# Graph convolution with a sparse adjacency on one core: the unit of the first columns comes two places later in the order of the units

## The chip, the cores and the metric

The kernel runs on one core of a Trainium2 chip. The metric is the device time of one execution in microseconds (us); the median of the runs counts.

## The reference

Only what matters of it is shown. There are 8 batches of 4096 nodes with 256 features; `adj` is 4096 x 4096 and sparse, denser towards the first rows and columns: the chance of an entry falls with the root of both indices.

```python
HW = jnp.einsum('bnf,fo->bno', H, W)
A_norm = jax.nn.relu((A + A.T) * 0.5)
D = jnp.sum(A_norm, axis=1)
D_safe = jnp.where(D > 0, D, 1.0)
d_inv_sqrt = jnp.where(D > 0, D_safe ** (-0.5), 0.0)
DAD = d_inv_sqrt[:, None] * A_norm * d_inv_sqrt[None, :]
L_norm = jnp.eye(N, dtype=H.dtype) - DAD
out = jnp.einsum('nm,bmo->bno', L_norm, HW)
return jax.nn.relu(out)
# around it: x = _layernorm(x + that, axis=-1)
```

## The kernel before

It has two halves. The first builds what the second multiplies; everything is in 32-bit floats.

**Building (lines 691 to 748).** The adjacency is read in blocks of 512 x 512, made symmetric with transposes on PE, cut at zero and written to `a_dram`. Beside it the features are multiplied by `w` and scaled with the root of the degrees; the result `g`, one row of 2048 values (8 KB: 8 batches of 256) for each node, goes to `g_dram`. A flag for each node and each group of 32 columns says whether there is an entry at all (`uses`). The product for the first 128 output rows (`lead`) is made here already.

**Multiplying (lines 885 to 1256).** The 31 other blocks of 128 output rows go in 16 *units*: unit `u` has the blocks 2u+1 and 2u+2, unit 15 only the last one. So unit 0 holds the first, densest columns after `lead`. For a unit only those rows of `g` are fetched that have an entry in its columns. They are sorted by *kind*, which is the pattern of the eight groups of 32 columns that a row has entries in; the tables `CAPS` and `FIRST` give each kind a number of half tiles of 64 rows, and the place of the first. This gives each unit its number of gathered tiles of 128 rows: 22, 19, 19, 18, 17, 17 and 16 for the units 1 to 7, 27 for unit 0, and 17, 16, 14, 15, 15, 13, 13 and 10 for the units 8 to 15.

`steps_of(u)` (line 818) makes the unit's list of PE steps. A full step multiplies a whole tile, or one of two fixed hub tiles of the first 256 nodes, into one block. A tiled step, or round, packs up to eight products of 64 rows by 32 columns, taken from up to five neighbouring tiles, side by side on the array. Both take four column slices of 512. Steps by unit: 21, 18, 17, 15, 15, 14 and 13 for the units 1 to 7, 28 for unit 0, and 12, 12, 12, 12, 11, 11, 11 and 4 for 8 to 15. A tile can be needed in several rounds.

What sets the order:

- `SEQ` (line 24) is the order of the units. `steps` (line 904) strings their steps together in it, and `order` (line 905) the tiles by first use.
- `gather(n)` (line 936) fetches tile n with two indirect DMAs on POOL's queue: the weights out of `a_dram` (line 943) and the rows of `g` (line 951; up to 1 MB). Tiles lie in a ring of `RING = 12` slots. `gather_ahead` (line 961) counts off slots strictly in order: a tile is gone only when all tiles before it are used up too, and its slot is what tile n + 12 waits for.
- While a unit runs, the lists of later ones are made: `ahead` (line 1083) takes, from the places two, three and four further in `SEQ`, the unit whose indices are spread out (`spread`), the unit whose leftover rows are placed (`place_rest`), and the unit whose patterns are found (`patterns`, `place`). This is DVE work with a few small matmuls in between (`lists`, line 1100), which stand in PE's order near the end of the unit.
- Each finished block is evicted from PSUM by ACT (line 759), added to its block of `x`, normalised on DVE and stored (line 812, SP's queue); the `x` blocks are loaded on ACT's queue (line 753). These start some steps into the next unit (`after`, lines 1199 to 1208).
- `queue(engine)` chains what each engine gets in the order of the program.
- In the building half `SEQ` gives the place at which the constants of each unit are set (line 648), and the first four units, whose lists are begun there (lines 730 and 737).

Of the kernel before, what the change touches and what calls it, by code (L numbers as in the profile page):

```python
# [20 lines left out]

KINDS = [15, 1, 4, 2, 8, 16, 64, 32, 128, 240, 51, 204, 60, 195, 0]

SEQ = [1, 2, 3, 4, 5, 6, 7, 0, *range(8, 16)]

HUBS = [*[2] * 15, 0]

# [40 lines left out]
def kernel(  # L68
# [49 lines left out]
    def blocks(u):  # L118

        return min(2, NB - 1 - 2 * u)  # L120
# [349 lines left out]
    with (  # L470
# [176 lines left out]

        due = [[n + 1, constants, (u,)] for n, u in enumerate(SEQ)]

# [29 lines left out]
        def spread_early(u):  # L679
            hot = spool.tile([P, A, S], F32, tag="sym", name=f"hot_{u}")  # L680
            mixed = blocks_pool.tile([P, A, S], F32, tag="adj", name=f"mixed_{u}")
            mixed = mixed.rearrange("p a s -> p (a s)")
            n = NB * tmax
            return spread(
                u,
                hot.rearrange("p a s -> p (a s)").bitcast(BF16).rearrange("p (m q) -> p m q", q=P),
                mixed[:, : n // 2].bitcast(BF16).rearrange("p (m t) -> p m t", t=tmax),
                mixed[:, n : 2 * n].bitcast(BF16).rearrange("p (m k t) -> p m k t", k=2, t=tmax),
            )

        for i in range(NS):
# [37 lines left out]
            if i in (1, 2):  # L729
                for n, u in enumerate(SEQ[2 * i - 2 : 2 * i]):  # L730
                    at = 1 + 5 * n
# [4 lines left out]
            elif i in (3, 4):  # L736
                pieces = spread_early(SEQ[i - 3])
                due += [[at, next, (pieces, None)] for at in (1, 2, 3, 3, 4)]
                due.append([5, collect_index, (SEQ[i - 3],)])
            due.sort(key=lambda d: d[0])  # L740
# [10 lines left out]
    def residual(i, engine):  # L751
        xr = blocks_pool.tile([P, B, F], F32, tag="adj", name=f"xr_{i}")
        engine.dma_start(xr, x[:, i * P : (i + 1) * P, :].rearrange("b p f -> p b f"))
        return xr
# [130 lines left out]
    with (  # L885
# [17 lines left out]
        stat = gath.enter_context(tc.tile_pool(name="stat", bufs=3))  # L903
        steps = [(u, step) for u in SEQ for step in steps_of(u)]
        order = list(dict.fromkeys((u, op[0]) for u, step in steps for op in step if op[0] >= 0))
# [81 lines left out]

        u = SEQ[0]
        xr = {i: residual(i, nc.sync) for i in (0, *range(2 * u + 1, 2 * u + 1 + blocks(u)))}
# [330 lines left out]
```

## Time and profile before

| | |
|---|---|
| median of 3 runs | 1507.45 us (1506.8 to 1508.42) |
| the profiled execution, its own time | 1505.85 us |
| its span, first to last instruction | 1503.7 us |
| mean granted clock of PE | 0.968 |
| indirect DMAs of rows of `g` (line 951) | 268 |
| moved by DMA | 543.04 MB, mean 361 GB/s |
| units, first product to last product | 591.7 to 1484.9 us |

The span is what the profile sees of the execution's own time; 2.2 us lie around it. PE is TensorE, PEld its weight loads, DVE VectorE, ACT ScalarE, POOL GpSimd and SP SyncE. A wait is written as the waiting instruction, an arrow, and who ended the wait. The DMA share is the mean busy share of 16 DMA engines; packets of several queues that overlap can put it a little over 1.

### The profile page before, as it was taken

To read this page: it belongs to the slowest core of one execution; us is meant where nothing else is said; L and a number is where in the kernel's file an instruction comes from. 1 tells how busy PE (TensorE), PEld (TensorE's weight loads), DVE (VectorE), ACT (ScalarE), POOL (GpSimd) and SP (SyncE) were. 2 spreads that over 40 slices of the span, in tenths; PEclk is the share of its full clock that TensorE was granted. 3 is DMA by queue.
4 is the path that set the end of the run, shared out by engine and by line. 5 is a ranking of instruction groups with operands and counts; after the bars stand their busy time and mean duration, and the time that the engine had idled before them with its cause. 6 is when DMAs were issued, how large, how long until landed. Compare 5 with 4: busy or idle time off the path is not lost.

```text
span 1503.7 us, 29689 instructions
## 1 busy us (share of the span) xinstructions
PE 1387.0 (92%) x11008; PEld 751.7 (50%) x11008; DVE 1040.8 (69%) x3173; ACT 361.2 (24%) x462; POOL 773.3 (51%) x1564
## 2 busy tenths in 40 slices
PE   6999998989999988999999999999999998988983
PEld 5877876767777763343433333333333333433431
DVE  5676668979956462319486897789229897999644
ACT  3555554444444451000101101100010010011111
POOL 3444010011213225775775777777566776777762
PEclk9999999999999989999999999999999999999996
DMA  9999999999989999999999999999979999999994
GB/s 358 366 364 398 399 376 360 367 330 354 356 311 348 332 397 379 394 400 332 373 379 358 375 398 379 382 388 384 366 255 343 343 374 401 374 368 391 379 370 144
DMA packets 217158, 543.04 MB, mean 361 GB/s; under 512 B 19369, under 2 KB 109193, under 8 KB 182425
## 3 DMA queue, kind: packets, MB, share of 16 engines
q0 software_dynamic: 55664, 283.87, 48.8%
q1 hardware_dynamic: 93472, 126.89, 24.6%
q10 hardware_dynamic: 67872, 130.32, 23.1%
q8 instruction: 89, 1.46, 0.4%
q14 instruction: 61, 0.50, 0.1%
HBM read 438.03 MB, written 136.34 MB: 382 GB/s over the span
## 4 chain that ended last, share of the span: by engine, by line
PE 52%; DMA 19%; DVE 19%; issue 5%; POOL 3%; ACT 2%; ACTq 0%; SPq 0%; POOLq 0%; DVEq 0%
PE py L1158 33%; DMA g<-g_dram,gi 9%; PE pg L606 9%; DMA a_dram<-sym 4%; DVE sym L499 3%; PE lead L564 3%; PE tr L495 3%; PE xtr L595 3%; DVE sums L506 3%; DMA ga<-a_dram,ai 2%; DMA xin<-in_x_dram 2%; DVE stats L778 1%; POOL ga L943 1%; DVE xr L769 1%; DVE xr L802 1%
## 5 line engine op out<-in xcount | busy, mean ns | idle before, releaser
L1158 PE MATMUL py<-g,ga 64*32 64x512 f32 (+1 forms) x7136 | 619.9, 609 | 29.1 <-DMA g<-g_dram,gi 24.8
L1158 PEld LDWEIGHTS py<-g,ga 64*32 64x32 f32 (+1 forms) x7136 | 226.9, 113 | 405.7 <-issue 323.2
L951 POOL DMA_INDIRECT g<-g_dram,gi x268 | 306.4, 1143 | 115.7 <-issue 67.4
L943 POOL DMA_INDIRECT ga<-a_dram,ai x268 | 285.9, 1067 | 137.4 <-PE py L1158 65.2
L759 ACT ACTIVATE y<-py,minus_r 128x512 f32<-128x512 f32 x120 | 72.8, 688 | 793.5 <-PE py L1158 562.8
L606 PE MATMUL pg<-w_sb,xt 128*128 128x256 f32 x1024 | 229.5, 382 | 5.8 <-ACT xt L596 4.0
L1158 PE MATMUL py<-g_hub,gh 128*128 128x512 f32 x480 | 222.1, 604 | 3.9 <-DVE pos_k L239 3.9
L499 DVE TENSOR_TENSOR sym<-tr,adj 128x512 f32<-128x512 f32 x256 | 161.5, 680 | 81.1 <-PE tr L495 80.1
L606 PEld LDWEIGHTS pg<-w_sb,xt 128*128 128x128 f32 x1024 | 194.0, 192 | 33.6 <-ACT xt L596 4.4
L507 POOL TENSOR_SCALAR uses<-sums 128x64 uint8<-128x64 f32 x64 | 27.7, 433 | 311.3 <-DVE sums L506 262.8
L506 DVE TENSOR_REDUCE sums<-sym 128x64 f32<-128x2048 f32 x64 | 145.3, 2276 | 51.7 <-ACT sym L503 51.7
L495 PE MATMUL tr<-ident,adj 128*128 128x128 f32 x1024 | 139.7, 287 | 28.6 <-DVE sym L499 16.6
L1158 PEld LDWEIGHTS py<-g_hub,gh 128*128 128x128 f32 x480 | 88.0, 190 | 132.7 <-issue 119.8
L503 ACT ACTIVATE sym<-sym 128x2048 f32<-128x2048 f32 x64 | 122.8, 1918 | 126.5 <-DVE sym L499 126.5
L495 PEld LDWEIGHTS tr<-ident,adj 128*128 128x128 f32 x1024 | 119.7, 147 | 55.3 <-DVE sym L499 34.1
L442 DVE TENSOR_SCALAR low<-lists 128x17 f32<-128x17 f32 (+8 forms) x14 | 2.5, 175 | 197.9 <-PE lists L430 193.3
L769 DVE TENSOR_TENSOR xr<-xr,y 128x2048 f32<-128x2048 f32 x31 | 70.8, 2284 | 52.7 <-ACT y L759 47.1
L595 PE MATMUL xtr<-ident,xin 128*128 128x128 f32 x512 | 73.9, 292 | 14.5 <-DVE sym L499 14.0
L802 DVE TENSOR_SCALAR xr<-xr,mv,root 128x256 f32<-128x256 f32 x248 | 85.6, 416 | 1.1
L778 DVE BATCH_NORM_STATS2 stats<-xr 128x6 f32<-128x256 f32 x248 | 84.1, 412 | 1.1
L564 PE MATMUL lead<-gt,strip 128*128 128x512 f32 x176 | 82.6, 593 | 0.0
L596 ACT COPY xt<-xtr 128x512 f32<-128x512 f32 x128 | 67.9, 593 | 45.1 <-PE xtr L595 44.0
(157 smaller groups left out, 1056.7 us busy)
## 6 DMA issues: line engine op xcount, KB each, us to landing
adj<-in_adj_dram SPq DMA_DIRECT2D x64, 1024.0 KB, 12.1
a_dram<-sym ACTq DMA_DIRECT2D x64, 1024.0 KB, 10.0
out_dram<-xr SPq DMA_DIRECT2D x31, 1024.0 KB, 17.5
xr<-in_x_dram ACTq DMA_DIRECT2D x28, 1024.0 KB, 18.4
xin<-in_x_dram SPq DMA_DIRECT2D x44, 512.0 KB, 10.5
g_dram<-gt ACTq DMA_DIRECT2D x22, 1024.0 KB, 7.6
xin<-in_x_dram POOLq DMA_DIRECT2D x20, 512.0 KB
g_dram<-held ACTq DMA_DIRECT2D x10, 1024.0 KB, 11.7
```

The costliest lines, as they stand in the source:

```text
L495: ins = nc.tensor.transpose(pt[:, c * P : (c + 1) * P], tji[:, c, a * P : (a + 1) * P], ident)
L499: nc.vector.tensor_add(sym[:, a, :], pt, tij[:, a, :])
L503: nc.scalar.activation(sym, sym, AF.Relu, scale=0.5)
L506: nc.vector.tensor_reduce(sums, sym.rearrange("p a (c q) -> p a c q", q=E), AX.X, ALU.add)
L564: nc.tensor.matmul(lead[c], lhsT=strip, rhs=g[:, c * S : (c + 1) * S], start=not done, stop=len(done) == NB - 1, skip_group_check=True,)
L595: nc.tensor.transpose(pt[:, k, c, :], xin[b // H][:, b % H + k, c * P : (c + 1) * P], ident)
L606: ins = nc.tensor.matmul(pg[:, k * FO : (k + 1) * FO], lhsT=xt[:, b + k, c, :], rhs=w_sb[:, c, :], start=(c == 0), stop=(c == FC - 1),)
L778: nc.vector.bn_stats(stats[:, b, :], z[:, b, :])
L802: nc.vector.tensor_scalar(z[:, b, :], z[:, b, :], mv[:, b, 0:1], rstd[:, b : b + 1], ALU.subtract, ALU.mult,)
L943: nc.gpsimd.indirect_dma_start(out=at if both else at[:, : E if one else P], out_offset=None, in_=a_pairs if both else a_groups if one els ...
L951: nc.gpsimd.indirect_dma_start(out=gt, out_offset=None, in_=g_dram, in_offset=bass.IndirectOffsetOnAxis(ap=gi[:, t : t + 1], axis=0), boun ...
L1158: return nc.tensor.matmul(py[2 * u + 1 + b][c][cols, :], lhsT=at[ps, off + cols.start : off + cols.stop], rhs=gt[ps, c * S : (c + 1) * S], ...
```

## The change

Unit 0 moves from the eighth place of the order to the tenth: the order was 1 to 7, 0, 8 to 15, and is 1 to 9, 0, 10 to 15. The units 8 and 9 come one unit 0 earlier, behind unit 7; behind unit 0 now stands unit 10. Nothing else is edited. Through `SEQ` this reorders the steps, the gathers, the preparation of lists and, in the building half, the place at which the constants of 8, 9 and 0 are set.

```diff
-SEQ = [1, 2, 3, 4, 5, 6, 7, 0, *range(8, 16)]
+SEQ = [*range(1, 10), 0, *range(10, 16)]
```

## The prediction

> **What bounds the kernel now.** I read the page first (busy time, slices, chain), then the stretches of the units, then the gap that these show, at its queue.
>
> The page says that no engine is free in the span as a whole:
>
> ```profile
> span 1503.7 us, 29689 instructions
> ## 1 busy us (share of the span) xinstructions
> PE 1387.0 (92%) x11008; PEld 751.7 (50%) x11008; DVE 1040.8 (69%) x3173; ACT 361.2 (24%) x462; POOL 773.3 (51%) x1564
> ```
>
> The change lies in the second half, from the first product at 591.7 us on. There I needed the units apart. L1158 has 7136 + 480 = 7616 matmul records and the list of steps has 952 products, so a product is 8 records; counted off in order of time, this gives the start of each step and unit: unit 7 at 967.4, unit 0 at 1019.7, unit 8 at 1122.5, 9 at 1172.8, 10 at 1221.4, 11 at 1274.3, 12 at 1323.0, then 13. Columns below: length, busy time of PE, PEld, DVE, ACT and POOL (instructions), PE clock, DMA share, GB/s.
>
> ```profile
> 967.40:1019.70 52.30, 49.72 (x398) 19.48 (x397) 45.34 (x171) 4.84 (x8) 38.72 (x37) 0.97 1.01 383
> 1019.70:1122.50 102.80, 101.35 (x862) 38.45 (x861) 44.93 (x171) 4.84 (x8) 66.38 (x65) 1.00 0.92 348
> 1122.50:1172.80 50.30, 46.15 (x565) 16.91 (x563) 45.95 (x172) 4.85 (x8) 33.21 (x32) 0.97 0.87 306
> 1172.80:1221.40 48.60, 44.86 (x452) 17.99 (x445) 44.28 (x168) 4.85 (x8) 36.58 (x35) 1.00 0.99 365
> 1221.40:1274.30 52.90, 48.43 (x509) 18.86 (x508) 41.98 (x157) 4.85 (x8) 36.94 (x36) 0.94 1.02 390
> 1274.30:1323.00 48.70, 43.65 (x467) 19.42 (x464) 44.86 (x169) 4.85 (x8) 36.97 (x35) 1.00 1.00 372
> ```
>
> Three limits in turn: unit 0 is PE's (101 of 103 us busy), units 7, 10 and 11 are the DMA engines' (share 1.00 and more), and DVE has 42 to 46 us of work in each unit however long it is. Units 0 and 8 are where the DMA share drops. A finer cut shows when:
>
> ```profile
> 1080.00:1100.00 20.00, 20.00 (x217) 7.32 (x223) 0.00 (x0) 0.00 (x0) 9.40 (x10) 1.00 0.72 268
> 1100.00:1120.00 20.00, 20.00 (x167) 8.08 (x152) 0.53 (x3) 2.42 (x4) 11.33 (x12) 1.00 0.90 315
> 1120.00:1130.00 10.00, 10.00 (x80) 3.77 (x79) 9.47 (x34) 2.42 (x4) 4.06 (x4) 1.00 0.37 116
> 1130.00:1150.00 20.00, 20.00 (x250) 7.37 (x254) 18.83 (x85) 0.00 (x0) 12.67 (x14) 1.00 0.98 318
> ```
>
> Unused DMA time: 0.28 x 20 + 0.10 x 20 + 0.63 x 10 = 13.9 us. Its cause stands in POOL's timeline: gathers wait until PE frees a ring slot.
>
> ```profile
> 1089.78 1.00 POOL L951 DMA_INDIRECT g<-g_dram,gi  x1 [7.87 <-PE py L1158]
> ...
> 1122.91 0.97 POOL L943 DMA_INDIRECT ga<-a_dram,ai  x1 [4.15 <-PE py L1158]
> ...
> 1129.96 0.97 POOL L943 DMA_INDIRECT ga<-a_dram,ai  x1 [2.73 <-PE py L1158]
> ...
> 1137.12 0.97 POOL L943 DMA_INDIRECT ga<-a_dram,ai  x1 [2.94 <-PE py L1158]
> ```
>
> And PE's waits in all name DMA first, then DVE:
>
> ```profile
> PE py L1158 <- DMA g<-g_dram,gi: 24.8, 14, 3.1
> ...
> PE lists L293 <- DVE kind L283: 6.0, 2, 3.4
> PE lists L430 <- DVE val L425: 5.8, 1, 5.8
> ```
>
> **What the Trainium skill says.** "DMA: Bandwidth & Descriptors", section "Issuing engines are not separate DMA queues": what SP, ACT and POOL issue interleaves on the same 16 engines. The trace agrees: from 1140 to 1150 us gathers held 0.49 of them, stores and loads of x 0.46 together. "Perfetto Trace Analysis", section "Optimization Strategy": where the contended engine changes over time, interleaving the regimes can help, and a repeated gap can mean too few buffers. Here the gap recurs only where the ring of 12 is full. "TensorE: Matmul & The Clock Gate", section "What's actually happening": an idle window of some 3.4 us lowers PE's clock. The trace agrees: unit 10, with waits of several us, has 0.94, and its step after them takes 3.96 us where others take 3.43.
>
> **The change part by part.** It permutes a list. No instruction, byte or product is added or taken; what is moved is unit 0 with all that it issues: 27 gathers on POOL with their weights, hub weights, two x loads on ACT, two stores on SP, its steps on PE, and the DVE work on its lists, which runs four, three and two places ahead.
>
> *Building phase (to 591.7 us).* The two places of the order from which lists are built there hold 1 to 4 in both orders. Only the constants of 8, 9 and 0 swap places: a few POOL memsets in a phase where POOL waits 262.8 us for DVE's sums. 0; even uncovered, it is the same memsets in another order. Units 1 to 7 of the second half: 0, except that in units 5 to 7 the lists in preparation are those of other units (unit 0's spread has 27 tiles where 16 or 17 are usual; the spread of 14 takes 0.62 + 0.62 + 0.41 us, so about 1.2 us more on DVE, once earlier and now in unit 8).
>
> *Balance of each unit.* PE: a step takes about 3.53 us, and the list matmuls 1.2. DMA: a gathered row of 8 KB occupies an engine 0.332 us, so 128 rows on 16 engines take 2.66 us; the weights add 0.2 a tile; x and out, 4 MB of 1 KB packets at 47 to 50 ns, about 12.3 us a unit. With the rows counted from packets between landings:
>
> - unit 0: 28 steps, 100 us PE; 23.6 full tiles, about 80 us DMA: PE-heavy by 20
> - unit 8: 12 steps, 43.6; 13.7 tiles, about 52: DMA-heavy by 8
> - unit 9: 12 steps, 43.6; 12.9 tiles, about 49: by 6
> - unit 10: 12 steps, 43.6; 13.3 tiles, about 50: by 6
>
> So unit 0 lets the gathers run ahead (its first tile landed 14 us before use, unit 8's first 36 us), the ring fills, and 13.9 us are thrown away.
>
> *What stays.* After the change unit 0 again follows a DMA-heavy unit (unit 10's first tile landed 12 us before use behind unit 9, about the 14 of unit 0 behind 7). The first 7.6 us of the loss hang on unit 0's own tiles and come again.
>
> *What changes at its end.* Slots are freed in order. Behind unit 0, unit 8 frees one slot after its second step (7 us), and the next only after its fourth, since its tiles 1 and 3 come back there (14.5 us): the waits at 1129.96 and 1137.12. Unit 10 uses its first four tiles in its second step alone, so four slots come free at 7 us. About two gathers, 2 x 2.8 = 5.6 us, go out up to 7 us earlier. Loads and stores already fill the engines from 8 us on (0.98), so only part is saved: from 0 to 5 us of DMA time; I take 3.
>
> *What follows on PE.* From list matmuls to list matmuls DVE needs 48.8 to 49.2 us where PE waited for it (1117.7, 1166.9; 1273.0, 1321.8), 45.6 in unit 12. Now:
>
> - units 8 and 9, without a lead: 50.4 + 48.6 become about 52 + 50 (their DMA need), +3
> - unit 0: waits for three late tiles as now, 102.8 to 105, +1
> - unit 10, with a lead: 52.9 becomes DVE's 49, -4
> - units 11 to 13: 48.7, 50.4 and 39.5 are DVE's and PE's, 0
> - units 14 and 15: 7 and 13 us above their bare steps, waiting for tiles; what the DMA engines are ahead comes out here, -4
>
> Sum +3 +1 -4 -4 = -4 us; the DMA side (3 us, bounds 0 and 5) agrees within its error. The profiled execution took 1505.85 us (2.2 around the span), which makes 1501.9; the median of the runs is 1507.45, 1.6 above it, so 1503.5.
>
> **The rivals.**
>
> *No change.* The whole 13.9 us are lost again behind unit 0, since x traffic would have covered what unit 10 frees early. For it: DMA share 0.98 right after the gap; total bytes equal, so that the end moves only by idle DMA time. Against: the unit behind now needs 14 tiles, not 17, and has nearly all in the ring. 1507, between 1504.5 and 1510.5.
>
> *A larger gain.* Unit 10's early slots count in full, and the list matmuls come in time, so units 10 and 14 run at their bare steps: -5 more, about 1498. Against it: DVE's 48.8 us.
>
> *Slower.* One mechanism: the lead thrown away sooner and three DMA-heavy units in a row. Units 6 and 7, of 17 and 16 tiles and no lead, took 55.8 and 52.3 us; if 8 and 9 do so too, they cost 5.4 + 3.7 = 9 us, and PE's pauses lower its clock. If unit 0's end wastes as much as before and the later units stay at DVE's pace, only 3 of it come back: +6, 1513.5. It decides once 8 and 9 together take over 105 us while the DMA idle time behind unit 0 is still 14 us or more. For it: in the trace unit 8, with all its lead, still ended waiting for tiles 15 and 16. Against: while PE waits, the DMA engines work, and the bytes done there are not to be done later.
>
> **How the numbers follow.** Forecast (-3 to -7 us) 0.38; larger gain 0.10; no change 0.22; slower 0.30. I hold 0.2%, 3 us, for what a measurement can tell. Faster 0.48, same 0.22, slower 0.30. The likeliest case alone: 1500 to 1505. Range for 8 in 10: from the larger gain, 1497, into the slower case, 1514.
>
> **What would show it.** Right: the same busy time of PE; DMA share 0.7 to 0.9 in the last 40 us of unit 0 and a low stretch at its end that ends after some 7 us; unit 10 below 50 us; 8 and 9 a few us longer; unit 15 shorter. Wrong: 8 and 9 at 55 us, a gap of over 14 us behind unit 0, or a change before 967 us.

## The result, and the profile after

The kernel after the change takes 1504.26 us (median of 14 runs, 1500.1 to 1508.94), the kernel before 1508.41 us in the same session (14 runs). The medians are 4.2 us apart. The ratio that the runs together give is 0.9965, with a 95% interval of 0.9952 to 0.9978, which is 5.3 us; 4 were forecast. A second measurement on another chip (below) gave 0.9971 (0.9962 to 0.9981).

The first lines of the page after (busy time of each engine) hardly differ from before:

```profile
span 1502.0 us, 29695 instructions
## 1 busy us (share of the span) xinstructions
PE 1384.2 (92%) x11008; PEld 752.1 (50%) x11008; DVE 1040.8 (69%) x3173; ACT 361.5 (24%) x462; POOL 772.0 (51%) x1564
```

The engines do the same work. From the first product to the last PE is busy for 847.4 of 893.2 us before and for 846.0 of 890.2 after, so it stands still for 45.8 and 44.2 us (42.0 in the second profile of the change, below). The gain is in good part time in which PE doesn't wait. The same stretches as in the prediction, now unit 8, 9, 0, 10 and 11 after the change (length, PE, PEld, DVE, ACT, POOL busy, PE clock, DMA share, GB/s):

```profile
1021.20:1074.80 53.60, 49.50 (x566) 18.77 (x564) 45.65 (x170) 4.85 (x8) 41.36 (x38) 0.94 0.97 368
1074.80:1127.20 52.40, 46.93 (x449) 18.70 (x446) 44.99 (x171) 4.85 (x8) 38.02 (x37) 0.97 0.96 354
1127.20:1230.30 103.10, 101.33 (x862) 38.50 (x861) 44.91 (x170) 4.84 (x8) 66.39 (x65) 1.00 0.93 357
1230.30:1275.00 44.70, 43.27 (x509) 18.66 (x508) 41.42 (x156) 4.84 (x8) 30.46 (x28) 1.00 0.91 341
1275.00:1324.50 49.50, 44.09 (x468) 19.88 (x464) 45.16 (x169) 4.85 (x8) 37.19 (x36) 0.97 0.98 367
```

Units 8 and 9 now run without a lead and take 53.6 and 52.4 us at a lower PE clock, and unit 10, behind unit 0, takes 44.7 where it took 52.9. These changes nearly cancel: the four units 8, 9, 0 and 10 take 254.6 us before and 253.8 after. The gain shows later. Units 14 and 15 of before, then of after:

```profile
1412.80:1458.10 45.30, 41.99 (x370) 17.29 (x369) 22.72 (x82) 6.60 (x11) 29.20 (x28) 0.96 1.00 382
1458.10:1484.90 26.80, 21.59 (x169) 6.71 (x167) 16.70 (x70) 0.72 (x2) 8.72 (x8) 0.81 0.68 242
```

```profile
1414.40:1454.30 39.90, 39.61 (x370) 15.68 (x369) 22.59 (x82) 6.63 (x11) 25.39 (x24) 1.00 1.01 384
1454.30:1483.30 29.00, 21.70 (x169) 7.22 (x167) 16.74 (x70) 0.69 (x2) 7.98 (x9) 0.82 0.70 251
```

Unit 14 is 5.4 us shorter, since PE works through (39.61 of 39.90 us, clock 1.00), and unit 15 is 2.2 longer.

| stretch | before, us | after, us | difference |
|---|---|---|---|
| units 1 to 7 | 428.0 | 428.2 | +0.2 |
| units 8 and 9 | 99.0 | 106.0 | +7.0 |
| unit 0 | 102.8 | 103.1 | +0.3 |
| unit 10 | 52.9 | 44.7 | -8.1 |
| units 11 to 13 | 138.5 | 139.4 | +0.9 |
| units 14 and 15 | 72.0 | 68.8 | -3.2 |

From the first product to the last it is 893.2 and 890.2 us, -3.0 (the lines are rounded). The building half of this one execution was 1.4 longer; one profile of the same kernel differs from the next by a few us, so the ratio of the runs, and not this difference, is the measure of the gain.

The stretch behind unit 0 that the prediction wanted shorter (columns as above; before it was the four windows from 1080 us on):

```profile
1190.00:1200.00 10.00, 10.00 (x136) 3.65 (x136) 0.00 (x0) 0.00 (x0) 2.42 (x3) 1.00 0.59 213
1200.00:1220.00 20.00, 20.00 (x171) 7.47 (x173) 0.00 (x0) 0.00 (x0) 14.64 (x15) 1.00 0.96 364
1220.00:1230.00 10.00, 10.00 (x72) 4.55 (x65) 2.77 (x12) 2.42 (x4) 2.52 (x3) 1.00 0.73 255
1230.00:1240.00 10.00, 10.00 (x79) 3.71 (x79) 9.45 (x35) 2.42 (x4) 5.49 (x5) 1.00 0.45 135
```

Unused DMA time: 0.41 x 10 + 0.04 x 20 + 0.27 x 10 + 0.55 x 10 = 13.1 us, against 13.9 (14.4 where before is cut at the same distances from unit 0's end). In the second profile of the changed kernel, below, it is 16.2 us, cut in the same way. So the gap did not shrink by what was forecast. POOL's timeline shows that the slots did come free as foreseen, four together after unit 10's second step, after two waits for PE:

```profile
1230.70 0.97 POOL L943 DMA_INDIRECT ga<-a_dram,ai  x1 [4.15 <-PE py L1158]
...
1237.75 0.97 POOL L943 DMA_INDIRECT ga<-a_dram,ai  x1 [3.01 <-PE py L1158]
...
1240.34 0.95 POOL L943 DMA_INDIRECT ga<-a_dram,ai  x1 [0.30 <-issue]
...
1242.92 1.83 POOL L943 DMA_INDIRECT ga<-a_dram,ai  x1 [0.30 <-issue]
```

What PE waits for in all, in the view of waits (us, times, longest), is hardly less than before (24.8 and 6.0):

```profile
PE py L1158 <- DMA g<-g_dram,gi: 23.9, 14, 3.4
PE lists L430 <- DVE val L425: 5.8, 1, 5.8
PE lists L293 <- DVE kind L283: 5.1, 2, 3.7
```

A better measure than the gap is the *lead*: by how much the first tile of a unit had landed before its first use. I took it from the issue and landing records of each gather.

| lead of unit | 8 | 9 | 0 | 10 | 11 | 12 | 13 | 14 |
|---|---|---|---|---|---|---|---|---|
| before, us | 36.2 | 16.4 | 13.8 | 12.5 | 20.0 | 21.9 | 21.0 | 15.4 |
| after, us | 13.9 | 15.0 | 14.3 | 35.4 | 23.6 | 24.2 | 22.8 | 19.3 |

In both kernels unit 0 makes a lead of about 36 us for the unit behind it. Unit 8 spends 20 of it in 50 us. Unit 10 spends 12 and hands on 23.6, and from there to unit 14 the changed kernel stays 2 to 4 us ahead. Unit 14 is where PE then no longer waits. The same in bytes: from unit 0's or unit 8's start at about 1020 us to the start of unit 11, 89.6 MB are moved in 254.6 us before and 90.2 MB in 253.8 after, counted from the packets. By estimate, 0.6 MB at unit 10's 390 GB/s of before are 1.5 us; with 0.8 of time that makes 2.3 of the 3.0 us.

### The profile page after: what moved, and what is told of

Read it like the earlier page. It is cut to its first block, busy times and chain, and to the rows that moved or that the text cites. A ratio compares the mean times of both kernels' runs of the same rounds, so it can differ in the third digit from the quotient of the medians.

```text
span 1502.0 us, 29695 instructions
## 1 busy us (share of the span) xinstructions
PE 1384.2 (92%) x11008; PEld 752.1 (50%) x11008; DVE 1040.8 (69%) x3173; ACT 361.5 (24%) x462; POOL 772.0 (51%) x1564
## 5 line engine op out<-in xcount | busy, mean ns | idle before, releaser
L951 POOL DMA_INDIRECT g<-g_dram,gi x268 | 301.4, 1125 | 117.1 <-issue 72.7
L943 POOL DMA_INDIRECT ga<-a_dram,ai x268 | 289.5, 1080 | 133.1 <-PE py L1158 61.2
L495 PE MATMUL tr<-ident,adj 128*128 128x128 f32 x1024 | 138.3, 284 | 29.1 <-DVE sym L499 16.7
L769 DVE TENSOR_TENSOR xr<-xr,y 128x2048 f32<-128x2048 f32 x31 | 70.9, 2286 | 53.2 <-ACT y L759 41.4
L595 PE MATMUL xtr<-ident,xin 128*128 128x128 f32 x512 | 72.2, 289 | 16.8 <-DVE sym L499 16.4
```

Source lines behind the costliest of these rows:

```text
L495: ins = nc.tensor.transpose(pt[:, c * P : (c + 1) * P], tji[:, c, a * P : (a + 1) * P], ident)
L943: nc.gpsimd.indirect_dma_start(out=at if both else at[:, : E if one else P], out_offset=None, in_=a_pairs if both else a_groups if one els ...
L951: nc.gpsimd.indirect_dma_start(out=gt, out_offset=None, in_=g_dram, in_offset=bass.IndirectOffsetOnAxis(ap=gi[:, t : t + 1], axis=0), boun ...
```

## The experiments

In the first five runs only the list `SEQ` differs, in the next two the ring has a slot less, in two the normalising is left out, and in three the order of the gathers is changed. Lines marked - are those of the kernel before.

**The change again.**

```diff
-SEQ = [1, 2, 3, 4, 5, 6, 7, 0, *range(8, 16)]
+SEQ = [*range(1, 10), 0, *range(10, 16)]
```

> The changed kernel once more, beside the runs below on one chip. If its gain is its own: 0.995 to 0.998 of before. If the first comparison was lucky and the order is worth no more than those of the first four runs: 0.999 to 1.001.

Measured: 1502.74 us against 1506.29, 0.9971 (0.9962 to 0.9981). Units 8 and 9 took 51.8 and 53.2 us, unit 10 44.7, unit 14 40.3: the picture repeats.

**Unit 0 left in its place, unit 10 behind it.** This has the follower of the change without the place.

```diff
-SEQ = [1, 2, 3, 4, 5, 6, 7, 0, *range(8, 16)]
+SEQ = [*range(1, 8), 0, 10, 8, 9, *range(11, 16)]
```

> Unit 0 stays in the eighth place, but unit 10 comes right behind it and 8 and 9 after that. Theory of the follower (a lead of gathers that unit 0 builds up is worth more before unit 10, which frees four ring slots at once after 7 us and has 14 tiles): the unit behind unit 0 takes about 45 us, the kernel about 0.997 of before, as with the change; unit 8, now without a lead, 53 us. Theory of the place (what counts is that 8 and 9 are done before unit 0): no gain, 1.000.

Measured: 1507.63 us against 1505.94, 1.0008 (0.9996 to 1.0021). Unit 10 took 45.8 us, but the kernel gained nothing. Units 0, 10, 8, 9 took 251.4 us, 3.2 less than before, and moved 88.5 MB, 1.1 less: the time was borrowed. Unit 8 got a lead of 25.0 us from unit 10, unit 9 17.9, and unit 11 12.8. POOL's timeline in unit 8 says how it was lost:

```profile
1181.27 1.00 POOL L943 DMA_INDIRECT ga<-a_dram,ai  x1 [1.03 <-PE py L1158]
...
1188.43 1.60 POOL L943 DMA_INDIRECT ga<-a_dram,ai  x1 [2.94 <-PE py L1158]
```

The gathers of unit 8's tiles 11 and 13 wait for the slots of its tiles 0 and 1 (free at 1181.0 and 1188.2). Since slots are given back strictly in order, later tiles that are used up earlier don't help. PE's own timeline shows it waiting for a tile and then for DVE:

```profile
1208.44 3.65 PE L1158 MATMUL py<-g,ga 64*32 64x512 f32 x60 [1.70 <-DMA g<-g_dram,gi]
...
1219.11 0.36 PE L293 MATMUL lists<-kind,ones 128*128 128x448 bf16 x1 [3.38 <-DVE kind L283]
```

**Unit 0 in the changed place, unit 8 behind it.** This has the place without the follower.

```diff
-SEQ = [1, 2, 3, 4, 5, 6, 7, 0, *range(8, 16)]
+SEQ = [*range(1, 8), 9, 10, 0, 8, *range(11, 16)]
```

> Unit 0 in the tenth place, behind 9 and 10, with unit 8 behind it. Theory of the follower: unit 8 takes about 50 us again, frees its slots late, and the gain is gone: 0.999 to 1.000. Theory of the place: 0.9965, as with the change.

Measured: 1506.73 us, 1.0000 (0.9986 to 1.0014). Unit 8 began with a lead of 34.8 us and took 49.9; unit 11 had 16.7. Unit 10, which here stands behind unit 9 and ahead of unit 0, took 46.0 us with a lead of 13.8, so it is not the lead from unit 0 that makes it short. No gain from the place alone either. What both runs share with the kernel before, and not with the change, is that unit 8 comes behind unit 0.

**Only unit 8 in front.**

```diff
-SEQ = [1, 2, 3, 4, 5, 6, 7, 0, *range(8, 16)]
+SEQ = [*range(1, 9), 0, *range(9, 16)]
```

> Unit 0 one place later than before, with unit 9 behind it, which frees two slots after 7 us and the next two only after some 21 us. Theory of the follower: between before and the change or no better than before, 0.998 to 1.000; unit 9 about 47 us. Theory of the place: half of the change's gain, 0.998, from unit 8 being in front.

Measured: 1505.75 us, 1.0006 (0.9993 to 1.0019). Unit 9 behind unit 0 took 48.9 us, unit 14 48.6. Half of the move brings nothing that could be measured; unit 9 behind unit 0 is no better than unit 8. The one profile taken here has 890.7 us from the first product to the last, as the changed kernel has, and the runs still show no gain: a single profile can't settle 3 us.

**Unit 0 later still, behind unit 12.**

```diff
-SEQ = [1, 2, 3, 4, 5, 6, 7, 0, *range(8, 16)]
+SEQ = [*range(1, 13), 0, *range(13, 16)]
```

> Unit 0 behind unit 12, with 13, 14 and 15 behind it. Theory of the follower: unit 13 uses its first four tiles once and frees four slots after 7 us, and units 14 and 15, which wait for tiles for 7 and 13 us before, get what is ahead: 0.993 to 0.996; units 8 and 9 again 53 and 52 us. Rival (DVE must rest): five short units 8 to 12 in a row without the long unit 0 between let DVE fall behind, their list matmuls wait longer than the 4 to 7 us seen, and the kernel is at 1.000 or slower.

Measured: 1503.17 us, 0.9978 (0.9967 to 0.9990). The gain is kept, not enlarged to the 0.993 to 0.996 expected: units 11 and 12, in front now, took 50.9 and 54.0 us (49.5 and 50.5 in the change), and in unit 14, 38.5 us long, PE was busy throughout. What comes at the end was paid in the middle. Unit 10, behind unit 9 here too, was short again:

```profile
1126.30:1171.20 44.90, 44.15 (x510) 18.69 (x508) 41.56 (x157) 4.84 (x8) 31.08 (x31) 1.00 1.01 390
```

**A ring of 11 slots, in both orders.** If slots are what binds, one less must cost.

```diff
-    RING = 12
+    RING = 11
```

> Order of before with a ring of 11 slots in place of 12. Supply theory (the end is set by when the last gathers land, and what POOL waits for ring slots is lost): POOL waits over 130 us for PE where it waited 96, and the kernel is 1 to 3% slower. Rival (POOL's waits for slots lie in times when the gathers are ahead anyway, and cost nothing): within 0.3% of before.

> Changed order with 11 slots. Supply theory: as much slower as the order of before with 11 slots or a little less, so that the changed order keeps its 0.2 to 0.5%. Rival (the gain hangs on the exact slot in which unit 10's tiles lie, that is on the ring's length): the gain is gone or turned at 11.

Measured: order of before 1518.55 us, 1.0082 (1.0062 to 1.0102); changed order 1518.01, 1.0076 (1.0054 to 1.0097). One slot of 1 MB is worth about 12 us, over twice the change, and with 11 the order's own gain can't be told from none: behind unit 0 the lead was 30.4 us in place of 35.4, and unit 14 took 47.8 us. The way in which the slot costs is not the expected one: POOL's waits for PE grew from 96.0 to 103.0 us in the order of before, and not to 130, and 0.8% is less than the 1 to 3% expected, while PE's waits for gathers grew from 24.8 to 32.7 us. A larger ring was not tried.

**Without the normalising, in the order of before.**

```diff
-                in_turn(normalise, i, z, mv, rstd)
```

> Order of before without the last eighth of DVE's work in the second half: the eight instructions of line 802 that scale and shift each block are left out for the blocks 0 to 30, so these come out unnormalised. 6.7 us less DVE work a unit. Theory that DVE's pace holds the later units (list matmuls 48.8 us apart): PE's waits for lists (13 us in all) go, units 11 and 12 take 44 instead of 49 and 50 us, and the kernel is 0.5 to 1% faster. Supply theory: PE's waits go over into waits for tiles, units 14 and 15 get longer, and the kernel stays within 0.3%.

Measured: 1506.42 us against 1506.29, 1.0004 (0.9992 to 1.0016). PE's waits, view of waits:

```profile
PE py L1157 <- DMA g<-g_dram,gi: 34.1, 17, 3.5
```

Left out are the instructions of line 802, 85.6 us of DVE's work or 5 to 6 a unit, so that the blocks are stored unnormalised. The two lines with DVE's lists are gone, and the wait for gathers has grown from 24.8 to 34.1 us. Units 8 and 12 are 5 to 6 us shorter, units 9 and 13 5 to 6 longer. So in this order DVE's pace decides where PE waits and not when the kernel ends. That the supply of gathers does fits, and so do the ends: the last 8 KB packet of a gather ended some 10 us before the last product (1474.6 and 1484.9 us before, 1473.3 and 1483.3 after, 1470.0 and 1479.9 with unit 0 behind 12).

**The gathers sorted by last use, and the change without normalising.** Four more kernels were to test the cause named in the second run. Of the tiles that are first needed in one step, those that are used up first are fetched first:

```diff
         order = list(dict.fromkeys((u, op[0]) for u, step in steps for op in step if op[0] >= 0))
+        first_use, last_use = {}, {}
+        for i, (u, step) in enumerate(steps):
+            for op in step:
+                first_use.setdefault((u, op[0]), i)
+                last_use[u, op[0]] = i
+        order.sort(key=lambda o: (first_use[o], last_use[o]))
```

> The order of the units of before; only the gathers are reordered: of the tiles that are first needed in the same step, those that are used up first are fetched first, in every unit. Unit 8 then has tiles 0, 2, 4 in its first three slots and frees three of them after its second step, where it freed one. Theory (a lead made in unit 0 is thrown away in unit 8, since slots are freed in order and unit 8 frees one at a time): unit 8 keeps some of its lead, tile 0 of unit 11 lands more than 24 us ahead of its use (20 before), and the run takes 0.997 to 0.9985 of before, some 2 to 5 us less, in the old order of the units. Rival (the sum of bytes and the pauses behind unit 0 set the end, not when slots come free inside a unit): 0.999 to 1.001, and the lead in unit 11 stays at 20 us.

> The change with the same reordering of the gathers. Theory: it adds to the change only what the other units throw away, unit 0 and units 11 to 13 among them, so less than it brings the old order if unit 8 was the main loser: 0.9945 to 0.9965 of before (the change alone: 0.9965). Rival 1 (no effect of the order of slots): 0.9965 as the change alone. Rival 2 (change and reordering are independent): the product of both ratios.

> Unit 0 behind unit 12, with the reordered gathers. Theory: nothing with a slow release of slots comes between unit 0 and the end, and the units in front lose less: 0.994 to 0.9965 of before (unit 0 behind unit 12 alone: 0.9978). Rival (the order of slots does nothing): 0.9978.

> The change without the normalising of the output blocks 0 to 30, which are stored as they are summed: that takes about 14 us of work off DVE in each unit. Theory (the supply of gathers sets the end, and DVE's pace only decides where PE waits): the change's gain is as large as with DVE's work, 0.9955 to 0.998 of before, as the old order without this work took 1.0004. Rival (DVE's 48 us from lists to lists hold back what the lead could bring, as the forecast argued against a larger gain): 0.991 to 0.994, and units 11 and 12 at 45 us or less.

These four ran together on a chip on which the kernel before itself takes 1756.58 us (19 runs), 17% more than elsewhere, so each can be held only against that time:

| kernel | us | ratio to before on that chip |
|---|---|---|
| order of before, sorted gathers | 1728.58 | 0.9848 (0.9806 to 0.9890) |
| changed order, sorted gathers | 1735.06 | 0.9874 (0.9836 to 0.9912) |
| unit 0 behind 12, sorted gathers | 1727.60 | 0.9833 (0.9796 to 0.9869) |
| changed order, no normalising | 1757.65 | 0.9996 (0.9974 to 1.0019) |

The building half is as elsewhere (first product at 592 to 596 us). The second half takes 1110 to 1142 us where 890 were usual. In the changed order without normalising, the 200 us from 1000 on (columns as above):

```profile
1000.00:1200.00 200.00, 159.22 (x1276) 55.35 (x1284) 103.74 (x419) 14.52 (x24) 104.58 (x104) 0.85 0.80 283
```

and PE at the end of unit 7, waiting four times within three steps:

```profile
1139.24 5.46 PE L1157 MATMUL py<-g,ga 64*32 64x512 f32 x64 [1.88 <-ACTq L1192]
1146.96 2.33 PE L1157 MATMUL py<-g,ga 64*32 64x512 f32 x16 [2.26 <-ACTq L1192]
1154.79 1.96 PE L1157 MATMUL py<-g,ga 64*32 64x512 f32 x16 [5.49 <-ACTq L1192]
1162.64 5.38 PE L1157 MATMUL py<-g,ga 64*32 64x512 f32 x48 [5.90 <-ACTq L1192]
```

L1192 is the tick in `tiled` (L1193 in the kernel before): with it ACT passes on that a group of PE's products is done, and the next group but one waits for that. The line below has all of PE's waits for ticks from 591 us on; in the kernel before, on an ordinary chip, they were 0.7 us.

```profile
PE py L1157 <- ACTq L1192: 199.7, 86, 9.4
```

Late gathers would be the obvious reason, but the trace speaks against it. The last two of the three steps need tiles 13 and 14 of unit 7, issued at 1128.8 and 1131.5 us. All 16 completions of tile 13's rows are on record by 1134.3, and PE's waits for the two tiles ended at 1139.3 and 1140.2, ahead of the three long waits. Unit 15, which takes 24.5 to 29.0 us elsewhere since it waits for tiles, takes 14.0 us in all four kernels here, the length of its four bare steps. In the ticks' records (1154.72 and 1162.58 us, each within 0.1 us of a product's end and of PE's next start) it is PE's own products that end late. No record shows why. Leads were not read here, since many completions of gathers are not recorded on this chip (866 on a semaphore that has 1347 in the trace of the same kernel without the move).

What follows. Fetching in the order of last use is faster by 1.5% on this chip, in the direction expected but far beyond the 0.15 to 0.3% that I had written. Since tiles are not what PE waits for there at the end, this doesn't show that the release of slots is the reason; how much of the 1.5% another chip would give is open. With sorted gathers the three orders can't be told apart, the changed order not even nominally ahead; that fits the reading that the order mattered through the release of slots, but it would also come out if the order simply brought nothing on this chip, and the change alone was not timed there. For the same reason the run without normalising decides nothing: 0.9996 lies outside what both theories expected (only its interval touches the first), and units 11 and 12 took 59.3 and 56.8 us. It also takes 5 to 6 us a unit off DVE and not the 14 that I had written. The sorted versions were below the time of before in every order on that chip; against the changed kernel on an ordinary chip they were not measured.

## Why the prediction was right

**The sign and the size.** Forecast -4 us of the profile, measured -3.0 in the second half of the two profiles and, by the runs, -4.2 (medians) to -5.3 (ratio). The likeliest case was the one that came. The sum is better than its terms: two of them were each off by 4 us, in opposite directions, and that they cancel is luck. Term by term:

- *Building phase and units 1 to 7, 0:* +1.4 (within what two profiles differ by) and +0.2. Right.
- *Units 8 and 9, +3:* they cost +7.0. I had priced them at their DMA need, 52 and 50 us, and left out that the waits fall unevenly in a unit and lower PE's clock (0.94 and 0.97). The slower rival's 105 us were passed, 106.0, and yet it didn't come. Its second condition, 14 us or more of idle time behind unit 0, was just missed here (13.1), but met in the second profile (16.2, with 105.0 us for the two units), and the kernel was no slower there either: the sign was a wrong one. Far more than its 3 us came back.
- *Unit 0, +1:* +0.3. Right.
- *Unit 10, -4:* -8.1, the term most in error. I set the unit's length to DVE's 49 us from list matmuls to list matmuls. That interval was what I said, 1225.51 to 1273.77, 48.3 us:

```profile
1225.51 0.35 PE L293 MATMUL lists<-kind,ones 128*128 128x448 bf16 x1
...
1273.77 0.36 PE L293 MATMUL lists<-kind,ones 128*128 128x448 bf16 x1 [1.43 <-DVE kind L283]
```

  but unit 0's lists stand 4.8 us before its end (1230.3) and unit 10's 1.2 before its own (1275.0), so that the unit between is 48.3 - 4.8 + 1.2 = 44.7 us. Nor was the lead the reason: behind unit 9, with a lead of 14 to 15 us, unit 10 took 46.0 us in the third run and 44.9 in the fifth. The 52.9 us of before hold waits that fall elsewhere in other orders. That the two errors, +4.0 and -4.1, are one, waits exchanged between units 8 to 10, is a reading and not shown.
- *Units 11 to 13, 0:* +0.9. Right.
- *Units 14 and 15, -4:* -3.2, though in unit 14 and not, as the list of signs had it, in 15.

**The cause.** "Slots are freed in order" and unit 10's four slots at once were right, and seen in POOL's waits. The step that failed is the one in which 3 us of idle DMA time were to be saved *in the gap behind unit 0*: the gap is 13.1 us (16.2 in the second profile) and was 13.9. Its agreement with PE's sum had no force. What the runs put in its place: the gap is made by unit 0 and stays, and the gain goes with how much of the full ring the next units keep. Unit 8 loses its lead wherever it comes behind unit 0, even with unit 10 between (the second run), and a place behind unit 0 is bad for unit 9 too (the fourth). In front of unit 0 they have little lead to lose, and the waits that they show there come back when unit 0, which is PE's, is followed by units that keep it. That neither the place nor the follower alone brings the gain is shown by the second and third run; the fifth has another place and another follower and keeps it, and shares with the change that both 8 and 9 stand ahead of unit 0. That the release of slots in order is the reason is not shown. It rests on unit 8's timeline, while the ring of 11 shows only that a slot is worth something, and the test made for it ended on a chip from which it can't be carried over. A rival stands beside it: units 8 and 9 have 17 and 16 tiles, units 10 and 13 only 14 and 13, for nearly the same number of steps, and a tile takes a whole slot however few of its rows are needed. No run separates the number of tiles from the order of their release.

**A reading that was wrong.** The prediction put unit 10's step of 3.96 us down to a lower clock. That step (1265.6 to 1269.5 us) ran at a granted clock of 1.00. The lower clock, 0.52, lies between 1252 and 1259 us, in the step that had just waited 3.1 us, and there most products took 1.06 us in place of 0.59. So the clock did fall after a wait, but in another step than the one named.

**The rivals.** *No change* was right on the gap and wrong on the end. *A larger gain*, held back by DVE's 48.8 us: unit 10 did run nearly at its steps (44.7 us, of 43.6), and taking 5 to 6 us of work a unit off DVE in the old order gave nothing, so the reason against it was the wrong one; a bound by the supply of gathers fits both. The Trainium skill's "Perfetto Trace Analysis", section "Optimization Strategy", which the prediction used for "too few buffers", agrees with the ring of 11: +0.8% for one buffer less.

## What to carry to other kernels

Where a ring of buffers feeds stages of different appetite, ask which stages come between the stage that fills the ring and the end: here the stages that needed many slots, and gave them back late because an early tile was used again, lost a lead that others kept. Do the accounts in leads and in bytes moved by a fixed place of the work, not in the lengths of single stages: a stage that gets shorter, or a wait that vanishes, can be a loan which a later stage pays back. A pace read from one mark to the next says nothing of a stage's length until one has looked where in each stage the mark stands.

## What the runs showed of the hardware that was not expected

The kernel before took 1505.9 to 1508.4 us (medians) in all sessions but one, and 1756.6 on that chip. A profile of the changed order without normalising there has the same bytes as the profiles elsewhere and nearly the same time for an 8 KB gather packet (344 ns mean, 332 before), and its building half is as fast. In the second half PE waits for 199.7 us for ticks that follow its own products (0.7 before), and the DMA engines' share falls to 0.80. In the case followed above the tiles had landed before those waits. No record shows the reason.
